# Layer-2 feed-forward of a macaron transformer: a token's six expert rows added on TensorE, shared features computed before the experts

## Chip, core and metric

The kernel runs on one core of a Trainium2 chip, as one program. The metric is the device time of one execution in microseconds (us), median over several runs. TensorE (PE in the profile; PEld is its weight load), VectorE (DVE), ScalarE (ACT), GpSimd (POOL) and SyncE (SP) each work through a queue of their own in order. SP, ACT and POOL can put transfers on DMA queues.

## What is computed

The network has four layers. Each layer is a feed-forward, an attention and the same feed-forward again, each behind a norm and with a residual: `x = x + 0.5 * ffn(norm(x))`, `x = x + attn(norm(x))`, `x = x + 0.5 * ffn(norm(x))`. The change lies in the feed-forward of layer 2, which is called twice:

```python
E, K, H, I, SI = 64, 6, 256, 96, 192
scores = jax.nn.softmax(xf @ gate_w.T, axis=-1)
topk_w, topk_idx = jax.lax.top_k(scores, K)
...
gx = xp[buf_tok]
gu = jnp.einsum('ech,ehi->eci', gx, gate_up_proj)
g, u = jnp.split(gu, 2, axis=-1)
hid = jax.nn.silu(g) * u
eo = jnp.einsum('eci,eih->ech', hid, down_proj) * buf_w[..., None]
routed = jnp.zeros((T + 1, h), x.dtype).at[buf_tok.reshape(-1)].add(eo.reshape(-1, h))[:T]
shared = jax.nn.silu(xf @ shared_gate_w.T) * (xf @ shared_up_w.T) @ shared_down_w.T
return (routed + shared).reshape(b, s, h)
```

Each of the 1024 tokens goes to 6 of 64 experts, and its result is the weighted sum of six expert rows plus the row of a shared expert that sees every token. All values are float32.

## The kernel before

The 1024 tokens lie in 8 tiles `x[t]` of 128 tokens by 256 features, which stay in SBUF. `m.norm()` makes the normed tiles and their transposes `xT` (two halves of 512 tokens). A tile framework takes the program, plans the order of each engine's queue from its own estimate of costs, and puts in all semaphores. Instructions that are traced earlier have precedence, but one that is traced later can be queued earlier where the planner sees an engine free and its operands ready.

`l2_ffn` runs in three stages.

Routing. `norm` (L165) writes the normed tiles to `xs`; the router's products go to one PSUM bank. VectorE picks each token's six experts, then ranks up to 64 tokens per expert in a long chain of maximum operations (L926, L928). Small products with the identity (L132, `lists` and `ps`) bring the ranks into two lists: `source`, the token behind each expert slot, and `target`, its row in the scratch tensor `parts`. The normed rows and the router's shares are written to a DRAM table (L922). In the second call the `beside` function is traced at the end of this stage: it loads and decodes the weights of layer 3 (L1482 onwards), with products on TensorE at L1532 and L1534 and copies on ScalarE at L1546 and L1555.

Experts. `experts(g)` handles four experts of 64 slots. It loads weights (SP, L964 and L970), gathers rows of the table with two indirect DMAs on POOL (L977, ten `rows` buffers), transposes them (L136), multiplies by the gate and up weights (L996), takes Silu (ScalarE, L1001), weights the features by the router's share (VectorE, L1006), transposes them, multiplies by the down weights (L132) and scatters the result rows to `parts` with two indirect DMAs on POOL (L1025). 16 such groups run staggered. `parts` holds a token's six rows side by side.

The end ("tail"). For each half, `m.gated` (L188) computes the shared expert's features: gate and up products of 96 by 512 outputs into `mm_bank` banks, Silu on ScalarE (L196), product on VectorE (L198). For each tile two products (`accb<-l_sd,hs`) give the shared row sums in an accumulator bank, and `add_to_x` (L204, VectorE) adds half of them to `x[t]`. After that SP loads the six rows of every token of a tile into `got` (L1043, 768 KB, 4 buffers, after all scatters), GpSimd adds rows 3 to 5 to rows 0 to 2 (L1049), and VectorE adds each of the three sums to `x[t]`. Then comes the norm of the next layer: layer 2's attention after the first call, layer 3's feed-forward after the second.

PSUM in this function has 8 banks: four of `mm_bank`, two for transposes (`tr_bank`), two accumulators (`acc_bank`).

## Time and profile before

| | |
|---|---|
| median of 6 runs | 2145.61 us (2143.31 to 2153.08) |
| the profiled execution | 2147.3 us |
| its span | 2145.6 us |
| mean granted TensorE clock | 0.903 |
| busy: TensorE / its weight load | 1844.1 us (86%) / 1196.5 us (56%) |
| busy: VectorE / ScalarE / GpSimd | 1198.4 us (56%) / 707.5 us (33%) / 578.0 us (27%) |
| first call: first gather, last scatter, last addition to `x` ends | 879.58, 984.30, 1023.93 us |
| second call: first gather, last scatter, layer 3's first product | 1798.29, 1904.24, 1943.34 us |
| `got` loads | 8 per call, 768 KB each |

Times of single events are us from the start of the span. A row of the timeline gives start, duration, engine, line, operation, what is written and read, shapes and count; in brackets stands how long the engine was idle before it and who released it. A group row gives count, then busy time and mean ns of one, then idle time and releasers. Row tiles such as `128*128 128x256` are the weights' shape and the output's shape. The ends of TensorE's instructions are modelled by the profiler, their starts are measured. "Granted clock" is the share of TensorE's full clock that its throttle let through.

### The profile page before, as it was taken

Reading aid. Unit: us, or ns where it says so; the run is one execution under the profiler, and the core shown is the slowest. Engines: PE = TensorE matmul, PEld = TensorE weight load, DVE = VectorE, ACT = ScalarE, POOL = GpSimd, SP = SyncE. Lnnn points to the kernel's source line nnn. Section 1 sums busy time; section 2 is a strip of 40 time slices with the busy share of each in tenths; the row PEclk is TensorE's granted clock in tenths of the full one; section 3 lists DMA queues with packets and bytes.
Section 4 is the critical chain, followed back from the end, with each engine's and each line's share of the span. In section 5 each row is a group of like instructions: output and inputs, shape, how many; then the busy total and the mean of one; then the engine's idle time right before and its main releaser. Section 6 shows DMA issues by size and latency. Waiting matters only on the chain. (4 is left out here: it accounts for less than half of the span.)

```text
span 2145.6 us, 33727 instructions
## 1 busy us (share of the span) xinstructions
PE 1844.1 (86%) x12924; PEld 1196.5 (56%) x12924; DVE 1198.4 (56%) x2910; ACT 707.5 (33%) x1573; POOL 578.0 (27%) x1128
## 2 busy tenths in 40 slices
PE   4979999998998998477668999999999968677878
PEld 2545555556656466343346667667677744344546
DVE  8553444333554433436788877687765652354563
ACT  7335512112553201111334554544545531110210
POOL 0023300001332000455334424434333322551110
PEclk9976899999998999678769999999999985887899
DMA  7000002252001213475120111111011064940000
GB/s 226 3 24 26 11 19 70 78 170 91 1 1 30 74 36 95 121 227 178 47 80 22 41 41 50 40 42 40 17 37 35 11 180 133 262 165 0 1 0 20
DMA packets 121872, 147.38 MB, mean 69 GB/s; under 512 B 18008, under 2 KB 95472, under 8 KB 121712
## 3 DMA queue, kind: packets, MB, share of 16 engines
q1 hardware_dynamic: 113488, 123.72, 19.6%
q0 software_dynamic: 6144, 18.88, 2.7%
q8 instruction: 103, 1.69, 0.3%
q10 hardware_dynamic: 2080, 2.62, 0.3%
q14 instruction: 57, 0.47, 0.1%
HBM read 120.03 MB, written 25.17 MB: 68 GB/s over the span
## 5 line engine op out<-in xcount | busy, mean ns | idle before, releaser
L132 PE MATMUL mmb<-xT,slot 128*128 128x512 f32 (+2 forms) x640 | 286.1, 603 | 2.1 <-DVE h L198 1.0
L132 PEld LDWEIGHTS mmb<-xT,slot 128*128 128x128 f32 (+2 forms) x640 | 118.1, 188 | 152.0 <-issue 145.1
L204 DVE SCALAR_TENSOR_TENSOR x<-accb,x 128x256 f32<-128x256 f32 x112 | 47.0, 421 | 197.9 <-PE accb L132 197.8
L132 PE MATMUL accb<-slot,h 128*128 128x256 f32 (+2 forms) x640 | 145.3, 384 | 0.0
L132 PEld LDWEIGHTS accb<-slot,h 128*128 128x128 f32 (+2 forms) x640 | 118.9, 190 | 28.7 <-issue 13.9
L1181 DVE SCALAR_TENSOR_TENSOR qT<-mmb,l_conv,qT 128x510 f32<-128x510 f32 (+2 forms) x96 | 70.8, 737 | 61.4 <-ACT qT L1177 60.5
L596 ACT ACTIVATE sg<-mmb 128x512 f32<-128x512 f32 (+1 forms) x56 | 33.4, 597 | 199.2 <-PE mmb L132 196.3
L1006 DVE SCALAR_TENSOR_TENSOR h<-sg,rows,mmb 64x96 f32<-64x96 f32 x128 | 40.1, 313 | 102.4 <-ACT sg L1001 83.1
L977 POOL DMA_INDIRECT rows<-table,source x64 | 61.9, 968 | 107.4 <-ACT l_ffn L1555 36.1
L144 ACT COPY xT<-trb 128x256 f32<-128x256 f32 x44 | 16.4, 372 | 215.3 <-PE trb L136 189.5
L1181 DVE SCALAR_TENSOR_TENSOR vT<-mmb,l_conv,vT 128x510 f32<-128x510 f32 (+2 forms) x96 | 71.1, 740 | 20.4 <-ACT vT L1177 19.5
L778 POOL TENSOR_TENSOR e<-e,den 128x512 f32<-128x512 f32 x64 | 51.6, 828 | 109.4 <-DVE den L775 106.3
L996 PE MATMUL mmb<-slot,gx 128*64 128x192 f32 x512 | 74.0, 414 | 6.4 <-DVE gx L142 4.0
L1025 POOL DMA_INDIRECT parts<-os,target x64 | 63.0, 984 | 33.8 <-issue 17.2
L1227 POOL TENSOR_TENSOR put<-lt,t_same 32x128 f32<-32x128 f32 x128 | 63.9, 499 | 26.5 <-DVE lt L1222 19.7
L726 POOL TENSOR_TENSOR x<-x,l_bo 128x256 f32<-128x256 f32 x8 | 6.5, 833 | 230.7 <-DVE xn L180 230.7
L598 DVE TENSOR_TENSOR sg<-sg,c 128x512 f32<-128x512 f32 x44 | 30.8, 700 | 67.0 <-ACT sg L596 47.9
L132 PE MATMUL mmb<-xT,wq 128*128 128x512 f32 x128 | 67.5, 652 | 0.0
L1181 DVE SCALAR_TENSOR_TENSOR kT<-mmb,l_conv,kT 128x510 f32<-128x510 f32 (+2 forms) x96 | 66.3, 734 | 1.9 <-ACT kT L1177 1.7
L132 PE MATMUL mmb<-xT,l_ffn 128*128 128x512 f32 x128 | 66.3, 663 | 1.2 <-DVE xT L142 1.2
L132 PE MATMUL accb<-wo,zT 128*128 128x256 f32 x256 | 61.8, 394 | 6.1 <-DVE x L204 4.5
L132 PE MATMUL mmb<-xT,wv 128*128 128x512 f32 x128 | 65.3, 634 | 0.0
(452 smaller groups left out, 4328.6 us busy)
## 6 DMA issues: line engine op xcount, KB each, us to landing
slot<-_L_ffn_gate_up_proj_dram SPq DMA_DIRECT2D x16, 1536.0 KB
slot<-in_L_ffn_down_proj_dram SPq DMA_DIRECT2D x8, 1536.0 KB
parts<-zero SPq DMA_DIRECT2D x16, 768.0 KB
got<-parts SPq DMA_DIRECT2D x16, 768.0 KB
bca<-scr SPq DMA_DIRECT2D x32, 256.0 KB
bcb<-scr SPq DMA_DIRECT2D x32, 256.0 KB
c<-rows SPq DMA_DIRECT2D x16, 256.0 KB
table<-xs ACTq DMA_DIRECT2D x2, 1280.0 KB
```

Source lines behind the costliest of these rows:

```text
L132: self.nc.tensor.matmul(out=out, lhsT=a, rhs=b, start=i == 0, stop=i == last, **kw)
L144: self.nc.scalar.copy(out, in_)
L204: self.nc.vector.scalar_tensor_tensor(self.x[t], got, scale, self.x[t], ALU.mult, ALU.add)
L596: nc.scalar.activation(sg[:n], g[:n], AF.Silu)
L598: nc.vector.tensor_tensor(sg, sg, c, ALU.mult)
L778: nc.gpsimd.tensor_tensor(e[:, :, cut], e[:, :, cut], den[:, i, :].unsqueeze(2).to_broadcast([P, 2, n]), ALU.mult)
L977: nc.gpsimd.indirect_dma_start(out=r, out_offset=None, in_=table, in_offset=bass.IndirectOffsetOnAxis(ap=slot[0][:, 2 * g + i : 2 * g + i ...
L996: nc.tensor.matmul(out=ps[half, i, :], lhsT=xT[:, i, k, half], rhs=gu[:, 4 * (g % 2) + 2 * i + j, k, :], start=k == 0, stop=k == KC - 1,)
L1006: nc.vector.scalar_tensor_tensor(h[half, i, :], sg[half, i, :], rows[i][half, D + e : D + e + 1], ps[half, i, 96:], ALU.mult, ALU.mult,)
L1025: ins = nc.gpsimd.indirect_dma_start(out=parts, out_offset=bass.IndirectOffsetOnAxis(ap=slot[1][:, 2 * g + i : 2 * g + i + 1], axis=0), in ...
L1181: nc.vector.scalar_tensor_tensor(yi[:, :, d:], ps[:, :, : S - d], tap(j), yi[:, :, d:], ALU.mult, ALU.add)
L1227: nc.gpsimd.tensor_tensor(batches[b].put[rows(q), :, :, u * G : u * G + G], lt[rows(q), :, rows(q)].rearrange("p c (z t) -> p t z c", z=2) ...
```

## The change

Three things change in `l2_ffn`. The shared expert's features of both halves are traced ahead of the experts and kept in `shared`. For each tile the accumulator bank collects the two shared products and six more products, with the identity as weights and each of the token's six rows as the moving operand; one `add_to_x` per tile takes the sum to `x[t]`. GpSimd's addition and the three additions of `got` on VectorE are gone. `got` has 5 buffers instead of 4.

```diff
         wk = pool("l2f", 2)
+        cols = lambda f: slice(f * 96, f * 96 + 96)
+        shared = [
+            m.gated(wk, half, lambda k, f: w.sg[:, k, cols(f)], lambda k, f: w.su[:, k, cols(f)], [96] * 2, "hs")
+            for half in range(2)
+        ]
         weights = {}
...
         staggered((experts(g) for g in range(16)), width=8, apart=1)
-        for half in range(2):
-            cols = lambda f: slice(f * 96, f * 96 + 96)
-            h = m.gated(wk, half, lambda k, f: w.sg[:, k, cols(f)], lambda k, f: w.su[:, k, cols(f)], [96] * 2, "hs")
-            for q in range(4):
-                o = m.acc_bank()
-                m.mm(o[:, :D], [(h[f][:96, q * P : (q + 1) * P], w.sd[:, f, :]) for f in range(2)])
-                m.add_to_x(half * 4 + q, o[:, :D], 0.5)
         for t in range(NT):
-            got = wk.tile([P, K, D], F32, name="got", bufs=4)
+            got = wk.tile([P, K, D], F32, name="got", bufs=5)
...
-            nc.gpsimd.tensor_tensor(got[:, :3], got[:, :3], got[:, 3:], ALU.add)
-            for k in range(3):
-                m.add_to_x(t, got[:, k], 0.5)
+            h, at = shared[t // 4], slice(t % 4 * P, t % 4 * P + P)
+            o = m.acc_bank()
+            m.mm(
+                o[:, :D],
+                [(h[f][:96, at], w.sd[:, f, :]) for f in range(2)] + [(m.ident, got[:, k]) for k in range(K)],
+            )
+            m.add_to_x(t, o[:, :D], 0.5)
```

## The prediction

> **What bounds the kernel now.** The changed function runs twice, so I read both stretches: the first call lies between 842 and 1032 us of the span, the second between 1735 and 1943 us. First I read the chain of waits (the page's fourth part, here in order of time: start, us, what) at the end of the second call.

> ```profile
> 1904.24 2.41 DMA parts<-os,target
> ...
> 1906.74 4.27 DMA got<-parts
> ...
> 1911.08 1.81 POOL got L1049
> ...
> 1913.37 1.92 DVE x L204
> ...
> 1928.49 1.67 DVE rs L157
> ...
> 1931.00 3.79 PE accb L132 x8
> ...
> 1943.34 16.73 PE mmb L132 x32
> ```

> From the last scatter (1904.24) the chain goes over the scatter's landing and the first load of `got` to 1911.0, and from there mostly over VectorE to 1943.34, where the layer-3 feed-forward begins on TensorE. That is 32.3 us, which I count from "T0", the first load's arrival (1911.0; in the first call 993.6). Next the groups of instructions in 1904 to 1944:

> ```profile
> L204 DVE SCALAR_TENSOR_TENSOR x<-got,x 128x256 f32<-128x256 f32 x24 | 17.2, 720 | 2.3 <-POOL got L1049 2.1
> L1049 POOL TENSOR_TENSOR got<-got 128x768 f32<-128x768 f32 x8 | 14.9, 1867 | 13.2 <-DMA got<-parts 11.8 <-DVE x L204 1.4
> L204 DVE SCALAR_TENSOR_TENSOR x<-accb,x 128x256 f32<-128x256 f32 x8 | 3.3, 417 | 0.9 <-PE accb L132 0.8
> ```

> The reader is to see the same VectorE operation at two prices: 417 ns when one operand comes from PSUM, 720 ns on average (up to 1.9 us) when it reads `got` while GpSimd adds. The stretch is bound by VectorE beside GpSimd, as the busy time by stretch says (length, then busy us of PE, PEld, DVE, ACT, POOL, granted clock, DMA share, GB/s):

> ```profile
> 1920.00:1930.00 10.00, 3.65 (x8) 2.35 (x8) 9.65 (x17) 0.00 (x0) 5.49 (x3) 0.58 0.67 232
> 1930.00:1943.00 13.00, 6.72 (x18) 3.78 (x16) 11.79 (x36) 0.74 (x2) 5.17 (x6) 0.50 0.05 22
> ```

> TensorE, now nearly idle there and at half clock, is what the change loads. Its prices, from the timeline (start, us, then idle before):

> ```profile
> 1904.78 1.88 PE L132 MATMUL mmb<-xT,l_sg 128*96 128x512 f32 x4
> ...
> 1931.00 3.78 PE L132 MATMUL accb<-l_sd,hs 96*128 96x256 f32 x8 [0.50 <-DVE x L204]
> ...
> 1943.34 16.73 PE L132 MATMUL mmb<-xT,l_ffn 128*128 128x512 f32 x32 [0.61 <-DVE xT L142]
> ...
> 1959.91 13.98 PE L132 MATMUL accb<-l_ffn,h 128*128 128x256 f32 x64
> ```

> A float32 product is two instructions here (64 rows for 4 tiles of 8 products). For 256 columns an instruction costs 13.98/64 = 0.218 us at full clock; at half clock 0.43. For 512 columns it is 0.43 (the next group of four starts 1.71 us later) and 0.86. After an idle time the half clock lasts 5.9 us at 1943.3 and about 2.9 us at 1031.9; I take 5 us.

> Last, the place where the shared expert's features go, the start of the experts in the two calls:

> ```profile
> 875.54 0.64 PE L132 MATMUL mmb<-q,t_flip 128*128 128x32 f32 x2 [0.28 <-DVE q L935]
> ...
> 883.15 0.66 PE L136 MATMUL trb<-t_ident,rows 128*128 128x128 f32 x2 [6.97 <-issue]
> ...
> 1796.17 1.22 PE L1534 MATMUL trb<-t_ident,floats 128*128 128x128 f32 x4
> ...
> 1801.66 0.66 PE L136 MATMUL trb<-t_ident,rows 128*128 128x128 f32 x2 [4.26 <-issue]
> ```

> TensorE stands idle for only 7.0 us (876.2 to 883.1) and 4.3 us (1797.4 to 1801.7) before the first gathered rows arrive.

> **The change, part by part.**

> *Features moved ahead of the experts.* Each call issues 32 instructions of 512 columns on TensorE (16 per half), 4 Silu on ScalarE (0.59), 4 products on VectorE (0.68), no DMA. In the old place, 1901.3 to 1908 and 1910 to 1919, they lay beside scatter, load and additions, so moving them frees nothing by itself. In the new place 5 us at half clock hold 5.8 instructions, the other 26.2 cost 11.3 us: 16.3 us. Behind them in TensorE's queue stand all the experts. In the second call they start at 1797.4 and end at 1813.7; the first group (transposes 0.66, copy 0.69, products 1.52, Silu 0.33, weighting 1.31, some 0.6 of hand-over, at full clock) has its features at 1818.8 instead of 1810.1: +8.7 us. GpSimd's eleventh gather needs a row buffer which that weighting frees, and the scatters stand behind the gathers in its queue, so the delay goes on to the last scatter. In the first call the same sum from 876.2 gives 897.6 instead of 891.7, +5.9; four instructions can use the bank that the router's sums left at 854, so I take 1.7 off: +4.2. ScalarE and VectorE wait there anyway.
> Bounds: no row shows when the planner puts these products on the queue. If all fit into the idle time of the routing (TensorE idle 862.8 to 874.8 and 1751.6 to 1761.1), the first group only gains from a warm clock: 889.3 for 891.7, -2.4, and about -1.5 in the second call. If nothing warms, 27.5 us less the idle 7.0 and 4.3: +20 and +23. I take the first sum, because before the change the features had their operands ready since 853 and yet did not fill the idle 7 us: banks seem to be given in the order of the program, and the routing's last three come first.

> *GpSimd's additions and the 24 additions of `got` per call removed.* 14.9 us of POOL and 17.2 us of DVE leave the tail. *Added:* six products per tile with the identity. With the two shared products a tile is 16 instructions of 256 columns: 3.49 us at full clock, then one addition of 0.42. Shared products of two tiles (two accumulator banks) run before T0, so 8 x 16 - 8 = 120 instructions remain: 11.6 in 5 us of half clock, 108.4 x 0.218 = 23.6, in all 28.6; the transposes of the first half (16 instructions, 0.66 per four) bring 31.0. TensorE becomes the bound of the tail at almost the old length: the loads came at 369 to 442 GB/s while buffers were free, 768 KB in about 2 us, faster than 3.49.
> First call: the last addition to x ends at T0+31.7; before it was 1023.9 = T0+30.3: +1.4. But the first half's norm is done some 10 us earlier, and the next layer's decay products (4.7 us at 1031.87) may fill TensorE's wait for the second half: between -4.7 and +1.4; I take -1, between them. Second call: layer 3 starts at T0+31.2 instead of 32.3 (-1.1), on a warm TensorE: 32 x 0.43 = 13.8 instead of 16.73 (-3.0): -4.1.

> [...] TensorE waits here from the last expert to T0, some 10 us. [...]

> *`got` from 4 to 5 buffers.* One load more ahead; nothing, since TensorE is the later one. Its cover is the 3.49 us per tile; at half clock even more so.

> **Sum:** 4.2 + 8.7 - 1.0 - 4.1 = +7.8 us. The profiled execution took 2147.3 us with a span of 2145.6, so it would become 2155.1; it lies 1.7 above the median of the six (2145.61), so against the median I expect 2153.4.

> **Rivals.**
> 1. *The features vanish in the routing's idle time* (the lower bound above): -2.4 - 1.5 - 1.0 - 4.1 = -9 us, 2136.6, faster. For it: 12 idle us beside the routing's VectorE work. Against it: the bank order, and that TensorE is busy 97% of 1776 to 1798. It decides once 8 us more of the moved products are hidden than I assume.
> 2. *The gathers hide the delay.* In both calls the second group's Silu comes 16.9 us after the first gather (896.53, 1815.23), whatever TensorE did. If that wait covers the features, the front costs 0 to 1 us and the tail's -5 remains: 2141 to 2146. Against it: those gathers wait for the first group's buffers.
> 3. *TensorE stays at half clock in the tail*: 51.6 us instead of 28.6, twice: +46 on the forecast, 2199. For it: 0.50 to 0.58 in the rows above; against it: with 3.5 to 6.9 us of work per load TensorE has no pause in which to cool.

> **Numbers.** Forecast 0.53, rival 1 0.25, rival 2 0.14, rival 3 0.08. The forecast's own range is 2147 to 2163. 0.2% (4.3 us) is about what a measurement of this kernel can tell from no change. Slower: most of the forecast and rival 3, 0.56; within: the edge of the forecast and half of rival 2, 0.15; faster: rival 1 and the rest, 0.29. The range reaches from rival 1's value to just over the forecast's: 2136 to 2164; the cold bounds of the front (+43 in all) and rival 3 lie outside, with under 0.15 between them.

> **What would show it.** In the profile after: 32 instructions on `l_sg` and `l_su` between the list products and the first transposed rows (right), or before 875 (rival 1); the time from first gather to last scatter longer by 4 and 9 us; in the tail TensorE busy nearly throughout at clock 1.00 after some 5 us, 0.22 us per instruction, VectorE under 60%, x's additions about 31 us after T0. A tail with pauses in TensorE, or a clock near 0.5 throughout, would make the sum wrong, as would an expert stage of unchanged length.

## The result, and the profile after

The changed kernel takes 2162.3 us (median of 20 runs, 2154.9 to 2175.8) beside 2145.8 us for the kernel before (46 runs): a ratio of 1.0071, 95% interval 1.0056 to 1.0087, that is +12 to +19 us. Its profiled execution took 2169.4 us with a span of 2167.7, seven above its own median, so single differences of a few us between the two profiles mean nothing by themselves. In particular, 9.7 of the 22 us between the two spans lie ahead of the first call, in code that is the same in both (the first write of `xs` comes at 851.8 instead of 842.2 us); the last section takes this up.

The features stand where the forecast put them. From the timeline of the changed kernel, second call (start, us, engine, line):

```profile
1819.78 3.62 PE L132 MATMUL mmb<-xT,l_sg 128*96 128x512 f32 x4
1820.88 1.08 POOL L982 DMA_INDIRECT rows<-table,source  x1 [36.06 <-ACT l_ffn L1557]
...
1839.40 1.31 DVE L1011 SCALAR_TENSOR_TENSOR h<-sg,rows,mmb 64x96 f32<-64x96 f32 x4 [1.57 <-ACT sg L1006]
1840.79 0.94 POOL L982 DMA_INDIRECT rows<-table,source  x1 [7.55 <-DVE h L1011]
...
1845.79 1.00 POOL L1030 DMA_INDIRECT parts<-os,target  x1 [0.30 <-issue]
...
1925.25 0.97 POOL L1030 DMA_INDIRECT parts<-os,target  x1 [0.30 <-issue]
```

The first group's weighting and the eleventh gather before, for comparison (first gather at 1798.29):

```profile
1808.80 1.31 DVE L1006 SCALAR_TENSOR_TENSOR h<-sg,rows,mmb 64x96 f32<-64x96 f32 x4
1810.93 0.95 POOL L977 DMA_INDIRECT rows<-table,source  x1 [0.30 <-issue]
```

TensorE is on `l_sg` and `l_su` before and while the first gathers run, the first group's weighting comes 18.5 us after the first gather (before: 10.5), and GpSimd's eleventh gather waits 7.55 us for it. But the last scatter ends 105.3 us after the first gather, and before it was 106.9: the stage did not get longer.

The tail of the second call, on TensorE, and the busy time by stretch (length, busy us of PE, PEld, DVE, ACT, POOL, granted clock, DMA share, GB/s):

```profile
1932.04 8.15 PE L132 MATMUL accb<-got,t_ident 128*128 128x256 f32 x24 [9.71 <-DMA got<-parts]
1940.03 1.03 PE L132 MATMUL accb<-l_sd,hs 96*128 96x256 f32 x4
1940.89 2.75 PE L132 MATMUL accb<-got,t_ident 128*128 128x256 f32 x12
...
1960.77 0.60 PE L136 MATMUL trb<-t_ident,xn 128*128 128x128 f32 x4
...
1963.83 13.97 PE L132 MATMUL mmb<-xT,l_ffn 128*128 128x512 f32 x32 [0.61 <-DVE xT L142]
```

```profile
1932.00:1940.00 8.00, 7.96 (x24) 6.60 (x25) 1.03 (x3) 0.00 (x0) 0.00 (x0) 0.65 0.96 372
1940.00:1950.00 10.00, 10.00 (x48) 8.76 (x48) 4.55 (x19) 0.00 (x0) 0.00 (x0) 1.00 0.66 220
1950.00:1964.00 14.00, 12.36 (x60) 10.36 (x59) 5.27 (x16) 0.74 (x2) 2.89 (x4) 1.00 0.00 0
```

TensorE has taken VectorE's place as the bound: busy without a pause, at full clock after some 6 us (0.65 on average over the first 8), 12 instructions in 2.6 us from start to start (0.217 each). Layer 3 begins 31.8 us after the first load's arrival (1932.04), on a warm engine: 13.97 us for the products that took 16.73. So neither call of the changed function is longer: from the first write of `xs` to the next layer's first product they take 189.8 and 205.6 us, before 189.7 and 207.5. The loss must lie elsewhere, in code that the change does not touch.

It lies in the attention between the two calls: 724.4 us from its first product to the transposes of the second call's `xs`; before 711.5. The busy time by stretch, first before, then after (columns as above, the granted clock third from the end):

```profile
1031.87:1743.36 711.49, 646.53 (x7529) 469.00 (x7529) 517.96 (x1094) 333.67 (x733) 268.86 (x738) 0.95 0.13 40
```

```profile
1041.59:1765.95 724.36, 649.52 (x7529) 472.90 (x7529) 518.23 (x1094) 333.44 (x733) 268.58 (x738) 0.94 0.13 40
```

Yet the queues of all five engines hold the same instructions there in the same order, 7528 of them product instructions of TensorE. What TensorE waited for in that stretch without any cause that the profile shows ("issue": total us, times, longest), first before, then after:

```profile
PE mmb L132 <- issue: 4.7, 3, 2.6
...
PE accb L132 <- issue: 0.3, 1, 0.3
```

```profile
PE mmb L132 <- issue: 8.4, 5, 4.1
...
PE mmb L136 <- issue: 1.7, 1, 1.7
...
PE accb L132 <- issue: 1.6, 1, 1.6
```

### The profile page after: what moved, and what is told of

Its sections match the earlier page's. It is cut to its first block, busy times and chain, and to the rows that moved or that the text cites. A ratio compares the mean times of both kernels' runs of the same rounds, so it can differ in the third digit from the quotient of the medians.

```text
span 2167.7 us, 34021 instructions
## 1 busy us (share of the span) xinstructions
PE 1884.4 (87%) x13116; PEld 1240.3 (57%) x13116; DVE 1165.4 (54%) x2862; ACT 707.9 (33%) x1573; POOL 547.8 (25%) x1112
## 5 line engine op out<-in xcount | busy, mean ns | idle before, releaser
L132 PE MATMUL mmb<-xT,slot 128*128 128x512 f32 (+2 forms) x640 | 286.3, 604 | 2.0 <-DVE h L198 1.0
L132 PEld LDWEIGHTS mmb<-xT,slot 128*128 128x128 f32 (+2 forms) x640 | 118.3, 189 | 152.0 <-issue 145.1
L204 DVE SCALAR_TENSOR_TENSOR x<-accb,x 128x256 f32<-128x256 f32 x112 | 47.3, 422 | 258.1 <-PE accb L132 258.1
L132 PE MATMUL accb<-slot,h 128*128 128x256 f32 (+2 forms) x640 | 145.3, 384 | 0.0
L132 PEld LDWEIGHTS accb<-slot,h 128*128 128x128 f32 (+2 forms) x640 | 118.8, 190 | 28.7 <-issue 13.9
L144 ACT COPY xT<-trb 128x256 f32<-128x256 f32 x44 | 16.3, 371 | 236.9 <-PE trb L136 211.1
L1001 PE MATMUL mmb<-slot,gx 128*64 128x192 f32 x512 | 65.6, 375 | 7.3 <-DVE gx L142 4.9
L1030 POOL DMA_INDIRECT parts<-os,target x64 | 63.0, 984 | 35.3 <-issue 15.9
L132 PE MATMUL accb<-got,t_ident 128*128 128x256 f32 x192 | 49.0, 411 | 22.7 <-DMA got<-parts 22.7
L132 PE MATMUL mmb<-xT,wq 128*128 128x512 f32 x128 | 68.7, 662 | 0.0
L1183 DVE SCALAR_TENSOR_TENSOR kT<-mmb,l_conv,kT 128x510 f32<-128x510 f32 (+2 forms) x96 | 66.3, 735 | 1.9 <-ACT kT L1179 1.7
L132 PE MATMUL accb<-wo,zT 128*128 128x256 f32 x256 | 62.0, 395 | 6.1 <-DVE x L204 4.5
L132 PE MATMUL mmb<-xT,l_ffn 128*128 128x512 f32 x128 | 64.6, 648 | 1.2 <-DVE xT L142 1.2
```

Source lines behind the costliest of these rows:

```text
L132: self.nc.tensor.matmul(out=out, lhsT=a, rhs=b, start=i == 0, stop=i == last, **kw)
L204: self.nc.vector.scalar_tensor_tensor(self.x[t], got, scale, self.x[t], ALU.mult, ALU.add)
L1001: nc.tensor.matmul(out=ps[half, i, :], lhsT=xT[:, i, k, half], rhs=gu[:, 4 * (g % 2) + 2 * i + j, k, :], start=k == 0, stop=k == KC - 1,)
L1030: ins = nc.gpsimd.indirect_dma_start(out=parts, out_offset=bass.IndirectOffsetOnAxis(ap=slot[1][:, 2 * g + i : 2 * g + i + 1], axis=0), in ...
L1183: nc.vector.scalar_tensor_tensor(yi[:, :, d:], ps[:, :, : S - d], tap(j), yi[:, :, d:], ALU.mult, ALU.add)
```

## What lies behind "issue": the program arrives in pieces

The profile's list of queues has one for instructions, of which the kernel before moves 103 packets and the changed one 104:

```profile
q8 instruction: 103, 1.69, 0.3%
```

```profile
q8 instruction: 104, 1.70, 0.3%
```

1.69 MB / 103 = 16.4 KB a packet. TensorE's records in the trace (weight loads, products, waits) are 26,321 before and 26,695 after, 102.8 and 104.3 times 256. I counted them from the start up to each of the stalls in the attention. A stall's length is taken from the start of one weight load to the start of the next. Here are those over 1.5 us, with their place in the program as whole pieces of 256 plus a rest:

```
kernel        stall  place            kernel                stall  place
before        2.8    35 x 256 + 193   identity only (e2)    4.0    35 x 256 + 193
                                                            2.3    36 x 256 + 193
                                                            1.8    42 x 256 + 193
                                                            2.1    47 x 256 + 194
                                                            2.2    66 x 256 + 193
                                                            1.6    76 x 256 + 193
                                                            1.9    82 x 256 + 193
```

```profile
1103.15 0.27 PE L132 MATMUL mmb<-inv,xs 32*32 32x16 f32 x5 [4.06 <-issue]
1106.60 0.53 PE L132 MATMUL mmb<-inv,lt 32*32 32x32 f32 x12 [1.53 <-issue]
```

A second loss goes with the stalls: the clock. In the attention TensorE ran at half clock for 77 us before and for 87 us after; in the second call's tail after, an instruction of 256 columns started every 0.43 us at half clock and every 0.22 at full.

In the attention TensorE's waits at these borders were up to 4.1 us long, and 16.2 us in all in the changed kernel, as the table below shows.

## The experiments

All stage lengths from the profiles in one table, to which the experiments refer. "Features" is the time from the first gather to the first group's weighting, "experts" from the first gather to the last scatter's end, "tail" from there to the next layer's first product, each for the two calls. "Place" is how many instructions later than before the attention's code lies, less whole pieces of 256. Stalls are the waits over 0.7 us at the border of a piece within the attention (number and sum), "half" the time at half clock there. The ratio is against the kernel before of the same group of runs, with its 95% interval. Groups, each on another chip: e1 to e4 (chip 0, before 2148.7 us), e5 to e8 (chip 3, 2143.2), e9 to e11 (chip 9, 2105.6), e12 (chip 10, 2101.2).

```
                       features    experts      tail       attention place stalls     half  ratio
before                 10.8 10.5  105.7 106.9  46.6 38.1   711.5       0   4,  6.0 us  77
changed                15.7 18.5  105.4 105.3  46.6 37.6   724.4     192   8, 16.2     87   1.0071 [1.0056, 1.0087]
e1 move only           16.1 17.4  109.8 109.1  43.9 32.0   709.6       0   3,  6.4     69   0.9963 [0.9936, 0.9990]
e2 identity only       11.6 10.6  105.7 106.4  46.5 42.3   725.5     192   8, 16.8     95   1.0090 [1.0059, 1.0121]
e3 first call only     16.2 10.6  106.2 104.4  46.8 38.4   720.9     192   9, 16.3     80   1.0102 [1.0067, 1.0138]
e4 second call only    10.9 18.4  106.2 104.4  45.9 37.9   704.9       0   2,  4.7     64   1.0004 [0.9976, 1.0031]
e5 before + 48 tiny    10.8 10.6  102.4 104.0  46.2 37.9   719.4     192   7, 14.3     86   1.0074 [1.0048, 1.0100]
e6 changed + 16 tiny   15.6 18.2  107.8 108.1  46.8 37.6   701.6       0   3,  5.9     60   1.0022 [1.0004, 1.0040]
e7 changed + 32 tiny   15.4 18.3  105.1 106.6  46.1 36.7   704.5      64   3,  5.8     67   1.0012 [0.9996, 1.0027]
e8 changed + 48 tiny   15.5 17.4  104.9 104.7  46.2 36.8   707.4     128   5,  7.9     67   1.0017 [1.0003, 1.0032]
e9 half on VectorE     16.1 18.4   88.0  90.5  36.6 28.4   712.4     128   6, 10.5     78   0.9969 [0.9945, 0.9994]
e10 half on GpSimd     16.1 18.4   87.8  90.9  40.1 32.4   712.5     136   6, 11.2     71   1.0012 [0.9987, 1.0036]
e11 move only again    16.2 18.3   87.5  91.1  43.6 31.9   705.7       0   3,  5.6     61   1.0003 [0.9981, 1.0025]
e12 two rows on TensorE 16.2 18.4  88.0  91.0  40.4 31.5   704.8      64   5,  9.9     64   1.0000 [0.9984, 1.0016]
```

One stall each in the changed kernel and in e3, e5, e7, e8, e9 and e12 (0.95 to 2.5 us) came 2.2 us or more after the packet had landed, so the fetch need not be its cause. e10 lies at 136 and not at 128 because TensorE's queue has eight waits more there.

### The change taken apart: its two parts, and its two calls

e1 keeps the move and puts the old additions back:

```diff
+        for t in range(NT):
+            h, at = shared[t // 4], slice(t % 4 * P, t % 4 * P + P)
+            o = m.acc_bank()
+            m.mm(o[:, :D], [(h[f][:96, at], w.sd[:, f, :]) for f in range(2)])
+            m.add_to_x(t, o[:, :D], 0.5)
...
+            nc.gpsimd.tensor_tensor(got[:, :3], got[:, :3], got[:, 3:], ALU.add)
+            for k in range(3):
+                m.add_to_x(t, got[:, k], 0.5)
```

> Only the move: the shared features of both halves ahead of the experts, GpSimd's and VectorE's additions of the rows as before, the shared sums directly behind the experts. Theory A (the delay of the first group goes on to the last scatter, as forecast): +4.2 and +8.7, that is +13 us on the kernel before, and the time from the first gather to the last scatter is 4 and 9 us longer. Theory B (the gathers cover the delay, as the profile of the changed kernel suggests: last scatter +0.1 and -1.4 us against the norm's first write): within 3 us of the kernel before. Theory C (the loss of about 16 us sits in the identity products): within 3 us too, and the next kernel then carries all of it.

Measured: 0.9963, 2 to 14 us faster; not +13. The first group is late by 5.3 and 6.9 us as in the changed kernel, and the first scatter by 1.1 and 2.6. In this profile the experts took 4.1 and 2.2 us longer, but the tails 2.7 and 6.1 us less. Theory A, with its delay added on undiminished, falls: the first call's 4.1 us alone would fit it, but in the second call it asks for 9 and there are 2.2, and the time is not longer. The tail's gain is something that the forecast had denied: without the features' work in it, the old way of adding is faster than before. The repeat e11 below has the same short tails but found no gain in time.

e2 puts the features back behind the experts and keeps the identity products:

```diff
         staggered((experts(g) for g in range(16)), width=8, apart=1)
+        shared = [
+            m.gated(wk, half, lambda k, f: w.sg[:, k, cols(f)], lambda k, f: w.su[:, k, cols(f)], [96] * 2, "hs")
+            for half in range(2)
+        ]
```

> Only the identity products: the features are computed behind the experts as before. The second half's 16 instructions of 512 columns then fall into the tail on TensorE, 16 x 0.43 = 6.9 us per call. Theory A: -1.0 - 4.1 + 2 x 6.9 = +9 us on the kernel before if nothing of them is hidden, -5 if the wait for the first load hides all. Theory C (TensorE in the tail costs more in most executions than the one profile shows, by cold clock): +15 us or more.

Measured: 1.0090, +13 to +26 us. That looks like theory C, but the table shows where the time is: the attention at 725.5 us. The tails are 46.5 and 42.3 us: the second half's features on TensorE lengthen the second by 4, the first not at all.

e3 and e4 make the change in one call alone (`new = beside is None`, and the opposite; the other call keeps the old code).

> The whole change in the first call alone, the second as before. Theory A: +4.2 - 1.0 = +3 us. Theory B with the loss behind the function (in the profile the attention between the two calls was 12.8 us longer though its instructions stand in the same order): +10 us or more. If that stretch was longer by chance alone: 0 to +1 us here.

> The whole change in the second call alone, the first as before. Theory A: +8.7 - 4.1 = +5 us. Theory B by the profile of the changed kernel (-1.9 to the layer-3 start, -2.8 on its first products): -5 us, and the attention between the calls unchanged. The two single-call kernels together should give the changed kernel's +16 us; if they don't, the loss needs both.

Measured: e3 +14 to +30 us, e4 -5 to +7. The whole loss needs the first call only, and in e3 it lies behind the changed function: its first call is 190.5 us long (before 189.7), its attention 720.9. e4, with the identity products and the moved features in the second call, has the attention as before. Nothing that the second call does costs anything that can be measured.

### Position of the code, with and without the change

e5 is the kernel before with 48 tiny products that nobody reads, in columns of an accumulator bank that are not used. They run in the routing stage, where TensorE mostly waits:

```diff
                 o = m.acc_bank()
+                for _ in range(48 if beside is None and half == q == 0 else 0):
+                    m.mm(o[:32, D : D + 16], [(m.ident[:32, :32], m.ident[:32, :16])])
                 m.mm(o[:, :D], [(h[f][:96, q * P : (q + 1) * P], w.sd[:, f, :]) for f in range(2)])
```

> The kernel before, with 48 tiny products with the identity (32 x 32 weights, 16 columns) into unused columns of one accumulator bank in the first call; nothing reads them, and nothing of the change is in. They add what the change adds to TensorE's queue ahead of layer 2's attention: 48 products, that is 192 instructions. Theory D (position of the code: TensorE's program comes in pieces of 256 instructions, its stalls 'issue' stand at one and the same place of each piece, and 192 more instructions ahead put that place onto other instructions of the attention): the attention takes about 723 us instead of 710.5, the time is +11 to +15 us, although the work added is under 5 us and stands where TensorE waits. Theory E (the memory plan with five got buffers, or TensorE's state after its busy tail, makes the attention longer): 0 to +3 us, attention at 710 us.

e6, e7 and e8 are the changed kernel with 16, 32 and 48 such products, traced in front of tile 0's sum in the first call (they too ran in the routing stage, between 840 and 849 us).

> The changed kernel, with 16 such tiny products in the first call: 64 instructions, so that the attention's code lies 192 + 64 = 256 instructions later than before, a whole piece. Theory D: the attention is back at about 710 us, and the time 11 to 15 us under the changed kernel's, 2146 to 2151 us beside a before of 2146. Theory E: no change against the changed kernel, +15 us on before.

> The changed kernel with 32 tiny products in the first call: the attention's code lies 320 instructions later, 64 beyond a whole piece. Theory D: an attention of a length of its own, between 700 and 730 us, with its 'issue' stalls at the same place of each piece. Theory E: as the changed kernel, 723 us.

> The changed kernel with 48 tiny products in the first call: 384 instructions, 128 beyond a whole piece. Theory D: again a length of its own between 700 and 730 us; with the kernels before, this gives the four positions in steps of 64. Theory E: as the changed kernel, 723 us.

Measured: e5 is 10 to 21 us slower than before, as slow as the changed kernel, with nothing of the change in it. e6, e7 and e8 do more work than the changed kernel and are within +1 to +9, -1 to +6 and +1 to +7 us of the kernel before. The waits of TensorE in the attention, first e5, then e6:

```profile
PE mmb L132 <- issue: 10.0, 6, 3.3
...
PE accb L132 <- issue: 1.5, 1, 1.5
```

```profile
PE mmb L132 <- issue: 5.9, 5, 3.0
```

By place, over all profiles: at 0 the attention takes 706.7 us (five profiles, 701.6 to 711.5) with 5.7 us of stalls and 66 us at half clock; at 192 it takes 722.6 us (four, 719.4 to 725.5) with 15.9 us of stalls and 87 us at half clock. That is 15.9 us, and of it 10.2 are longer stalls (9.1 without those that came late after their packet); 20.5 us more at half clock are worth at most another 10.2. At 64 it takes 704.5 and 704.8, at 128 707.4 and 712.4, at 136 712.5. Theory D is shown by both signs: the position alone makes the loss, and putting the position back takes it away. Theory E is out: e6 to e8 have the same five buffers and the same busy tail. The stalls' part is thus shown in the traces; that the clock follows on them is an inference from their going together in the means, and it holds only loosely (e10 has 11.2 us of stalls and 71 us at half clock, the kernel before 6.0 and 77).

The ratios agree with it. At place 192 they are 1.0071, 1.0090, 1.0102 and 1.0074, on average +18 us; e4, e6, e7 and e8, with the change in one call or both but another place, stand at 1.0004 to 1.0022, on average +3.

### Which engine should add the rows

With e1's tail in mind I divided the six rows: in e9 TensorE takes rows 0 to 2 with the shared sums and VectorE the others; in e10 GpSimd first folds six rows into three; e11 repeats e1 beside them; e12 leaves only two rows to TensorE. The core of e9 (e12 has 2 in place of 3, and no tiny products):

```diff
+                [(h[f][:96, at], w.sd[:, f, :]) for f in range(2)] + [(m.ident, got[:, k]) for k in range(3)],
             )
             m.add_to_x(t, o[:, :D], 0.5)
+            for k in range(3, K):
+                m.add_to_x(t, got[:, k], 0.5)
```

> Features ahead; TensorE adds rows 0 to 2 to the shared sums by products with the identity, VectorE adds the sum and rows 3 to 5 to x, GpSimd adds nothing. 8 tiny products in the first call put the attention's code 24 x 4 + 8 x 4 = 128 instructions later, a position at which it took 707 us. Per tile TensorE has 10 instructions of 0.218 = 2.2 us instead of 3.5, VectorE 4 additions of 0.42 = 1.7 us, a load takes some 2 us. By the tail sum of the prediction, 8 x 1.3 = 10 us less per call than in the changed kernel where nothing else holds it: 2132 to 2138 for a before of 2146. If the tail is held by the loads or by the norm behind it, some 5 us per call: 2138 to 2144.

> Features ahead; GpSimd adds rows 3 to 5 to rows 0 to 2 as before, TensorE adds the three sums to the shared sums, VectorE makes one addition per tile. Same position of the attention's code (128 later). GpSimd needs 1.87 us per tile, TensorE 2.2, VectorE 0.42, but they stand behind one another: a tile comes some 1.9 us later than in the kernel with half on VectorE. So 2 to 4 us more than that one.

> The move alone once more, beside the two kernels above. It adds no instruction on TensorE, so all code from the first call's end on lies as before. If the gain of 8 us was real: 2137 to 2142 for a before of 2146, with tails (last scatter to the next layer's first product) of about 44 and 32 us as in its first profile, against 46.6 and 38.1 before.

> Features ahead; TensorE adds rows 0 and 1 to the shared sums, VectorE adds the sum and rows 2 to 5 to x, nothing on GpSimd, no tiny products. 16 products more per call are 64 instructions: the attention's code lies where it took 704.5 us (64 past a whole piece), against 712 in the kernel with half on VectorE. Per tile TensorE 8 x 0.218 = 1.7 us, VectorE 5 x 0.42 = 2.1 us, about as long a tail as there (36.6 and 28.4 us behind the last scatter, against 46 and 38 in the kernel before). With the attention at 705 us the time is 10 to 14 us under the kernel before; if the position is worth nothing here, 5 to 7 us under it.

In these two groups the kernel before took 2105.6 and 2101.2 us instead of 2143 to 2149, and the experts 88 and 91 us where e1, the same kernel as e11, took 110 and 109. Each group ran on a chip of its own; whether that is the reason is not shown. The ratios stand within a group. Measured: e9 is 1 to 12 us faster than before, as the lower of its two expectations said, e10 and e12 the same, e11 the same (-4 to +5). So e1's gain is not reproduced. e9 is the only new kernel that is faster than before, by 0.3%; its interval ends no further from 1 than e1's did, and it was not repeated. Its tails are 7.0 and 3.5 us shorter than those of e11. The groups of instructions in the second call's tail (count, busy us and mean ns of one, idle time and releaser), e11's counterpart e1 first, then e9, then e12:

```profile
L204 DVE SCALAR_TENSOR_TENSOR x<-got,x 128x256 f32<-128x256 f32 x21 | 14.4, 685 | 7.9 <-POOL got L1052 7.6
```

```profile
L132 PE MATMUL accb<-got,t_ident 128*128 128x256 f32 x48 | 13.0, 416 | 9.7 <-DMA got<-parts 9.7
L204 DVE SCALAR_TENSOR_TENSOR x<-got,x 128x256 f32<-128x256 f32 x24 | 10.3, 430 | 0.3
```

```profile
L204 DVE SCALAR_TENSOR_TENSOR x<-got,x 128x256 f32<-128x256 f32 x32 | 13.3, 421 | 0.2
```

Beside GpSimd VectorE's addition costs 685 ns and waits 7.6 us for GpSimd; without it 430 and 421. In the profiles e9 gives all of this back elsewhere: its attention, at place 128, took 6.7 us more than e11's, its layer 3 1.2, its second routing 2.5. e12 has the good place, as expected (704.8), but VectorE's five additions per tile bind its tail, 3.8 and 3.1 us longer than e9's: the expectation of an equal tail was wrong, and so was that of a time 5 us or more under the kernel before. e10's tails are 3.5 and 4.0 us longer than e9's and its median 6.3 us, more than the 2 to 4 us expected. e9's division at place 0 or 64 was not tried.

## Why the prediction was right, and where it was not

The direction and the range held, but by luck: the terms of the sum make about nothing by what was measured, and nearly all of the loss comes from a term that the sum did not have. The prediction itself said that an expert stage of unchanged length would make the sum wrong, and this is what came. Forecast +7.8 us, measured +15.2 (0.0071 x 2146), and the two have little in common:

| term | forecast | measured |
|---|---|---|
| first group late, call 1 and 2 | +4.2, +8.7 | +4.9, +8.0 in the profile |
| carried on to the last scatter | the same | -0.3, -1.6 in the profile; +1.5, +1.0 over all |
| tail, call 1 | -1.0 | 0.0 |
| tail, call 2, and warm start of layer 3 | -1.1 and -3.0 | -0.5 and -2.8 |
| position of later code | not there | about +15 |

"Over all" compares the first three groups' profiles: features ahead 106.5 and 106.4 us (six each), behind 105.0 and 105.4 (four each). Single profiles scatter from 102.4 to 109.8, so these means exclude the forecast's +8.7 in the second call clearly and its +4.2 in the first less so.

**The step that failed** is "so the delay goes on to the last scatter". The features did stand in front and the first group was as late as computed. But the stage has slack behind that point, as the second rival said: the second group's Silu, 16.9 us after the first gather in both calls before, came 17.4 and 20.2 us after it, and the first scatter only 0.7 and 3.7 us later than before; at the end nothing was left in the profile. Rival 2 should have been the forecast for the front. The evidence, a Silu that does not move with TensorE, was in the prediction; I weighed it below an argument about buffers that was true of the sixth group, whose gathers came 4.4 and 7.3 us later than before. In the first call no gather of a later group came more than 1.3 us late; in the second they came 2.0 to 5.1 us late up to the fifteenth group, and at most 0.5 in the sixteenth.

The slack is not a property of the kernel alone. In e9 (chip 9) each group's gathers follow the previous group's by an even 5.1 to 5.2 us from the eighth group on, and the second call's extra delay is passed on whole: the sixth group's first gather comes 17.5 and 19.8 us after the call's first, the sixteenth's 66.3 and 68.6, and the last scatter ends after 88.0 and 90.5. e10, e11 and e12 show the same (2.1 to 2.3 us, passed on from gather to gather), and e11 is the kernel of e1. Where the gathers run evenly, the forecast's step may therefore hold. No profile of the kernel before was taken on those chips, and why the gathers came more slowly and unevenly on the others was not tested.

**The tail was sized well.** (The 31.0 us of its sum are 31.2, that is 28.6 and 2.6 for the transposes; the prediction goes on with 31.2.) Forecast: last addition 31.7 us after the first load, layer 3 31.2 us after it, first products 13.8 us; measured 29.0 in the first call, then 31.8 and 13.97. Clock and price per instruction, and VectorE at 29% (11.2 us of 39 from 1925 to 1964), are as said. For the first call's tail the value taken, -1.0, was too good; no gain came, because the first half's transposes came only after the last tile's products (1033.5 us).

**"Moving them frees nothing by itself" was wrong.** e1 shows tails 2.7 and 6.1 us shorter with the features gone. It did not enter the sum, since the new tail was computed directly, but it means that the identity products lose to the old additions by 2.7 and 5.6 us in the same place, 46.6 for 43.9 and 37.6 for 32.0.

**What no rival contained** is the code's position. The four terms of the changed function make some -1 us by the measured values (+1.5, +1.0, 0.0, -0.5, -2.8), and 1 to 5 us by the ratios of e4 and e6 to e8, in which e6 to e8 carry about 1.4 us for their tiny products (the first routing took 38.8 to 39.0 us instead of 37.4). Without the position the change would have been no change within about 0.2%. What the position does to layer 3, whose code lies 384 instructions later, was not separated: its length varied between 198 and 207 us without a pattern.

## What to carry to other kernels

When a change alters the number of instructions on an engine and the time moves in code behind it whose instructions are the same, compare that stretch instruction by instruction, and look at where the "issue" waits stand in the program. Padding with a few idle instructions to a whole piece told the change's own worth from its position's here: 16 tiny products took the ratio from 1.0071 to 1.0022 (e6). Where short instructions follow one another as densely as in this attention, try the position itself: the attention took 706.7 us at place 0 and 722.6 at 192. And a delay at the head of a staggered pipeline can be covered by the wait that comes next: in the changed kernel's second call the first group was 8.0 us late and the experts 1.6 us shorter, while on chip 9 the extra 2.3 us of e9's second call went through to the last scatter (88.0 and 90.5 us). Look for an event that already comes later than the delayed engine would need.

## What the runs showed of the hardware

At the changed kernel's first two stalls the packets of pieces began 3.35 and 3.45 us apart (1100.95, 1104.30 and 1107.75), although TensorE went through the 256 instructions between the two stalls in 1.7 us (1103.15 to 1104.81). The half-clock stretches of the profiles before and after last 3.4 us (11 and 10 of them) or a multiple of it (6.8, 10.2, 13.7, up to 41.0 in the kernel before), but for the one that the end of the span cuts off (0.7 and 0.1); they fall differently in the two. The stretch before the first call, with the same code in every kernel, took 841 to 842 us in twelve of the profiles and 851 to 852 in two, the changed kernel's and e5's: in its first 840 us the changed kernel was at half clock for 129.7 us, the kernel before for 109.2. That is 20.5 us more at half speed, worth at most 10.2. e2 and e3 lie at the same place as the changed kernel and e5 and are among the twelve, so the place does not make this difference. And the same expert code took 110 us on chip 0 and 88 on chip 9 (e1, e11), which no profile explains.
